# Latents' queries and keys turned by VectorE and transfers, zeros of the experts' rows moved into the context steps

## Chip, cores and metric

One core of a Trainium2 chip runs one program for one layer. The metric is device time of the run in microseconds (us), as the median of several runs. Everything is float32. The engines are named as the profile names them: PE is TensorE (PEld its weight loads), DVE is VectorE, ACT is ScalarE, POOL is GpSimd, SP is SyncE, whose queue issues nearly all transfers (SPq in the profile).

## What is computed

A perceiver layer with 256 latents `x` of 512 channels and 4096 context tokens: attention of the latents over context and themselves, then a state-space block, then a mixture of experts.

```python
x = x + xattn(layernorm(x), ctx)     # 16 heads, 4 key/value heads, head size 128
x = x + ssd(layernorm(x))            # state-space block
x = x + experts(layernorm(x))        # 32 experts, the best 6 for each token, and a shared one

# xattn, with x already normed:
q, k, v = x @ wq, x @ wk, x @ wv                 # by heads
k_ctx, v_ctx = ctx @ wk_ctx, ctx @ wv_ctx
q, k = rope(rms_norm(q, q_w)), rope(rms_norm(k, k_w))
k_ctx = rms_norm(k_ctx, k_w)                     # no rope
scores = q @ concat(k_ctx, k).T / sqrt(128)      # causal among the latents
out = softmax(scores) @ concat(v_ctx, v) @ wo
```

## The kernel before

**Attention is held turned.** A score product takes a block of 128 keys, `kT` (128 channels on the partitions, 128 keys), as the stationary side and the queries of four heads, `qT` (128 channels, 4 x 128 queries), as the moving side. Projections give rows by token: `ps_self` for the latents, `ps_k` and `ps_kv` for the context. So each 128 x 512 block of queries or keys has to be turned, head by head, before it can be used.

**Two arms.** A small test of the norms' weights selects between `layer(lctx, True)` (`bounded`: scores are small enough for an exponential without a running maximum) and a general arm. With the inputs of this case the bounded arm runs, and only it is meant below.

**First stage, to about 84 us.** After the loads of the first weights come the projections of context block 0 (four pieces of 128 tokens; `ctx_k`, `ctx_v`, turned by `ctx_t`) and of the latents: two blocks of keys (`k_of`), two of values (`self_value`) and eight of queries (`q_of`: four groups of four heads, j, by two blocks of 128 latents, t). The tuple that begins in L486 writes their order out by hand. `self_block` makes one block of keys or queries: `project` on TensorE into `ps_self`; in `norm_rope` a copy `raw` by ACT (L432), squares for the norm on ACT (`head_squares`, L247), four VectorE operations for the rotation (L437 to L440), a power on VectorE and POOL (`power_half`, L188 and L189), and a multiplication by POOL (L441) into `o`, which lies in the room of `lacc`. `self_block` returns a function `turn` (L467, L468) that turns `o` by four TensorE transposes into one PSUM bank `selfT` and copies it by ACT into `qT` or `kT0`. Turns are called later, when more than two are waiting in the list `turns`; the last ones are called three scores into the attention.

**Buffers.** In the bounded arm the pool `ps_tp` has one PSUM bank (tag `tp`), used by the turns of the latents (`selfT`) and of context block 0 (`kTp`). The SBUF pool `krp` has two buffers for each tag. Tag `sq` is shared by the squares, which nobody reads (only their sums are used), and by `tr` of the context keys.

**Context steps.** `bounded_attention` goes through s = 0 to 8. Step 0 is the latents' attention to themselves (12 scores; query block 1 sees both key blocks). After the last score of a group the queries are scaled in place by ACT (L597). Steps 1 to 8 are attention to context blocks 0 to 7, with 32 scores each. Each score is a product `scT` (L542), an exponential on ACT to `prT` (L545), a sum on VectorE (L553) and, two scores later, a value product `oT` (L562). On the diagonal of step 0 VectorE also masks `prT` (L548). Beside the scores of step s the keys and values of the next context block are made: `fast_steps(s)` returns 14 pieces, those of `row(1)` and then those of `row(0)`, and `bounded_attention` spreads them evenly over the scores. Two pieces of each row end with `key_blocks`, which turns a finished block of context keys without TensorE: VectorE turns all 32 x 32 blocks in one instruction (L284), four transfers put them into DRAM (`kd`, L286), each block at its turned place, and a fifth reads `kT` back (L288).

**Zeros.** The experts' rows are gathered in DRAM in `xg`, whose unused rows must be zero, and parts of `ye` and `ye2` must be as well. `clear(n)` writes a seventh of `xg` from a zeroed row block of `xn` (L501); `clear(0)` also the parts of `ye` and `ye2` (L505). `clear(s - 1)` is called at the beginning of step s.

**Order.** The instructions of an engine run in the order that a scheduler lays down while compiling: by priority, which follows the program's order, among those that its own estimate of times takes as ready. An instruction that has nothing to wait for can so come far ahead of its place in the program: the zeros are called in steps 1 to 7, and SP issues them from 31.8 to 79.1 us. `tc.keep_in_program_order(i)` puts i behind the instruction that the program has last given to the same engine.

Of the kernel before, what the change touches and what calls it, by code (L numbers as in the profile page):

```python
# [11 lines left out]
FP = mybir.dt.float32  # L12
# [7 lines left out]
P = 128  # L20
L = 256
NT = L // P
DM = 512
# [4 lines left out]
NH = 16  # L28
NKV = 4
REP = NH // NKV  # L30
HD = 128
# [9 lines left out]
SH = 16  # L41
# [5 lines left out]
NE = 32  # L47
# [9 lines left out]
TAIL = 6  # L57
# [10 lines left out]
def perceiver_layer(ctx: ExitStack, tc: tile.TileContext, a: dict, out: bass.AP):  # L68
    nc = tc.nc
    V, S, G, TE = nc.vector, nc.scalar, nc.gpsimd, nc.tensor  # L70
# [48 lines left out]
    xg = tc.dram_tile((ROUNDS * NE * P, DM), FP, name="xg")  # L119
    ye = tc.dram_tile(((NE + 1) * P, DM), FP, name="ye")  # L120
    ye2 = tc.dram_tile(((NE + 1) * P, DM), FP, name="ye2")
    kd = [tc.dram_tile((CK // P, NKV, HD, P), FP, name=f"kd{c}") for c in range(NC)]
    sums_d = [tc.dram_tile((SH, P), FP, name=f"sums{t}") for t in range(NT)]

    rope = const.tile([P, NT, 2, HALF], FP, name="rope")
# [7 lines left out]
    def layer(ctx, bounded):  # L133
# [6 lines left out]
        xn = keep.tile([P, NT, DM], FP, name="xn")  # L140
# [67 lines left out]
        def project(ps, lhs, rhs_of):  # L208

            for k in range(KD):  # L210
                TE.matmul(ps, lhs(k), rhs_of(k), start=(k == 0), stop=(k == KD - 1))  # L211
# [8 lines left out]
        krp = pool("krp", 2)  # L220
        ps_tp = pool("ps_tp", 1 if bounded else 2, space=PSUM)
# [19 lines left out]

        def head_squares(raw):

            sq = krp.tile([P, REP, HD], FP, tag="sq", name="sq")
            ss = small.tile([P, REP], FP, tag="ss", name="ss")
            for h in range(REP):
                S.activation(sq[:, h, :], raw[:, h, :], AF.Square, accum_out=ss[:, h:h + 1])  # L247
            return ss

        def key_rms(raw, r):  # L250

# [10 lines left out]
        def context_tiles(c):  # L262

            kT = kvp.tile([P, NKV, CK], FP, tag="kT", name="kT")
            v = kvp.tile([P, CK // P, NKV * HD], FP, tag="v", name="v")
            r = small.tile([P, CK // P, NKV], FP, tag="rk", name="rk", bufs=2)
            kv[c + 1] = (kT, v, r)
            raws = {}

            def key_transpose(i):  # L270
                tp = ps_tp.tile([P, NKV, P], FP, tag="tp", name="kTp")
                raw = raws.pop(i)
                for h in range(NKV):
                    TE.transpose(tp[:, h, :], raw[:, h, :], ident)

                if bounded:
                    S.copy(kT[:, :, i * P:(i + 1) * P], tp)
                else:
                    S.activation(kT[:, :, i * P:(i + 1) * P], tp, AF.Copy, scale=kw_col)

            def key_blocks(i):

                tr = krp.tile([P, NKV * HD], FP, tag="sq", name="tr")
                V.transpose(tr, raws.pop(i).rearrange("p h d -> p (h d)"))  # L284
                for b in range(0, P, 32):
                    nc.sync.dma_start(kd[c][i, :, :, b:b + 32].rearrange("h (j a) k -> a h j k", a=32),  # L286
                                      tr[b:b + 32, :].rearrange("a (h j k) -> a h j k", h=NKV, k=32))
                nc.sync.dma_start(kT[:, :, i * P:(i + 1) * P], kd[c][i].rearrange("h d k -> d h k"))  # L288
            return v, r, raws, key_transpose, key_blocks

        def context_pieces(c):
# [137 lines left out]
        def norm_rope(ps, t, tb):  # L429
# [11 lines left out]
            G.tensor_tensor(o, o, r.unsqueeze(2).to_broadcast([P, REP, HD]), ALU.mult)  # L441
            return o

        kT0 = kvp.tile([P, NKV, CK], FP, tag="kT", name="kT0")
        v0 = kvp.tile([P, CK // P, NKV * HD], FP, tag="v", name="v0")
        kv[0] = (kT0, v0, None)
# [12 lines left out]
        def self_block(t, w, tb, dst):  # L459
            ps = ps_mm.tile([P, 512], FP, tag="mm", name="ps_self")  # L460
            project(ps, lambda k: xT[:, k, t * P:(t + 1) * P], lambda k: w[:, k, :])
            o = norm_rope(ps.rearrange("p (h d) -> p h d", d=HD), t, tb)

            def turn():
                tp = ps_tp.tile([P, REP, P], FP, tag="tp", name="selfT")
                for h in range(REP):
                    TE.transpose(tp[:, h, :], o[:, h, :], ident)  # L467
                S.copy(dst, tp)  # L468
            return turn
# [24 lines left out]

        G.memset(xn[:, 0, :], 0.0)

        def clear(n):

            per = -(-ROUNDS * NE // (NC - 1))
            e0, e1 = n * per, min((n + 1) * per, ROUNDS * NE)  # L500
            nc.sync.dma_start(xg[e0 * P:e1 * P, :].rearrange("(e p) d -> p e d", p=P),  # L501
                              xn[:, 0:1, :].to_broadcast([P, e1 - e0, DM]))
            if n == 0:
                for y in (ye, ye2):
                    nc.sync.dma_start(y[(NE - TAIL) * P:, :].rearrange("(e p) d -> p e d", p=P),  # L505
                                      xn[:, 0:1, :].to_broadcast([P, TAIL + 1, DM]))

        nc.sync.dma_start(by_channel, a["by_channel"])
        nc.sync.dma_start(by_head, a["by_head"].partition_broadcast(P))
# [16 lines left out]
        def bounded_attention(beside):  # L526
# [50 lines left out]
            for s in range(NC + 1):  # L577
                if s < NC:
                    steps = [(s, g, t, i) for g in range(NKV) for t in range(NT) for i in range(len(keys_of(s, t)))]
                else:  # L580
                    steps = [(s, g, t, i) for t in range(NT) for g in range(NKV) for i in range(len(keys_of(s, t)))]
                    last_weights()
                extra = []
                if 0 < s < NC:
                    if s + 1 < NC:
                        load_ctx(s + 1)
                    clear(s - 1)
                    extra = fast_steps(s)
                done = 0
                for n, st in enumerate(steps):  # L590
                    if s == 0 and n == 3:
                        for turn in turns:
                            turn()
                    pending.append((*st, scores(*st)))
                    if s == 0 and st[3] == len(keys_of(s, st[2])) - 1:
                        q = qT[:, st[2], heads4(st[1]), :]
                        S.activation(q, q, AF.Copy, scale=kw_col)  # L597
                    if len(pending) > 2:
                        values(*pending.pop(0))
                    if s < NC:  # L600

                        while done < min(len(extra), len(extra) * (n + 1) // (len(steps) - 4)):
                            extra[done]()
                            done += 1
                    elif n > len(steps) // NT + 1:
                        for f in beside():
                            f()
# [103 lines left out]
        m = {}  # L711
# [6 lines left out]
        def mamba_memory():  # L718
            m["lm"], = carve(ctxp.tile([P, CK // P, KD, P], FP, tag="ctx", name="lm"), (SH, P))
            m["w_bcd"], = carve(ctxp.tile([P, CK // P, KD, P], FP, tag="ctx", name="w_bcd"), (KD, CK))  # L720
            nc.sync.dma_start(m["w_bcd"][:, :, 0:272], a["W_inT"][:, 2048:2320].rearrange("(k p) n -> p k n", p=P))
            for t in range(NT):
                m["csT", t] = krp.tile([P, REP, HD], FP, tag="sq", name="csT")[0:SH, 0, :]
            off = [krp.tile([P, REP, HD], FP, tag="kn", name="off") for _ in range(2)]
            m["off"] = ring([o.rearrange("p h d -> p (h d)") for o in off])
            gu = krp.tile([P, REP, HD], FP, tag="kraw", name="gu")
            m["sh"] = krp.tile([P, REP, HD], FP, tag="kraw", name="sh").rearrange("p h d -> p (h d)")
            for t, (tag, shape) in enumerate((("kT", [P, NKV, CK]), ("v", [P, CK // P, NKV * HD]))):
                tl = kvp.tile(shape, FP, tag=tag, name=f"xc{t}")
                names = ("vdt", "nab", "u", "z", "z2", "ser", "dt", "dA", "acs", "ea", "decay", "e1")  # L730
                m["xc", t], *sm = carve(tl, (XCT, P), *[(SH,)] * len(names))
                m.update({(n, t): v for n, v in zip(names, sm)})
                m["gu", t] = gu[:, t, :]
                m["kv", t] = tl
            m["xraw"], = carve(lacc[:, 0], (XCT, P + CONV - 1))
            m["zs"] = wvc.rearrange("p (t k) n -> p t (k n)", t=NT)
            m["xt"] = wkc.rearrange("p (t k) n -> p t (k n)", t=NT)
            m["xdt"], = carve(ctx0, (NT, DI))

            m["xdd"], m["s0"], m["y", 0], m["yT", 0] = carve(qT, (DI,), (DI,), (DI,), (DIT, P))  # L740
            m["y", 1], m["yT", 1] = carve(qT, (DI,), (DIT, P))
            G.memset(m["xraw"][:, :, 0:CONV - 1], 0.0)
            S.activation(m["ea", 0], a_log, AF.Exp)
# [522 lines left out]
        with ExitStack() as rctx:  # L1266
# [37 lines left out]
            for n in range(NP):  # L1304
# [27 lines left out]
                else:  # L1332
                    e0 = 2 * n - (NE - TAIL)
# [95 lines left out]
```

## Time and profile before

| | us |
|---|---|
| median of 3 runs | 1018.16 (1018.09 to 1018.35) |
| the profiled execution, its own time | 1019.19 |
| its span in the profile | 1017.40 |
| TensorE busy | 996.1 (98%) |
| VectorE busy | 495.4 (49%) |
| ACT busy | 384.6 (38%) |
| POOL busy | 156.9 (15%) |

The granted TensorE clock is full throughout (0.998). The span is cut into 40 slices of 25.4 us; the first four hold the loads, the latents' projections and step 0, the context steps follow up to slice 28, then the state-space block and the experts. In the lists of instructions, `x40` means that 40 of a kind are counted together; "idle before" names what ended the time in which the engine stood still. Starts are microseconds from the start of the span.

### The profile page before, as it was taken

How to read it: one execution, taken by the hardware profiler on the slowest of the kernel's cores; microseconds unless marked ns; L12 is line 12 of the kernel's file. 1: busy time of each engine (PE TensorE's matmuls, PEld its weight loads, DVE VectorE, ACT ScalarE, POOL GpSimd, SP SyncE). 2: the span in 40 equal slices, each digit the busy share in tenths (PEclk: the TensorE clock that was granted, in tenths of full speed). 3: DMA queues.
4: the chain of work that ended last, by engine and by line, in shares of the span. 5: the costliest groups of instructions: out<-in, count | busy, mean ns of one | idle time of the engine just before them, and what ended most of it. 6: DMA issues, size and time to landing. Idle time of an engine off the chain costs nothing.

```text
span 1017.4 us, 9099 instructions
## 1 busy us (share of the span) xinstructions
PE 996.1 (98%) x2818; PEld 480.9 (47%) x2818; DVE 495.4 (49%) x975; ACT 384.6 (38%) x870; POOL 156.9 (15%) x156
## 2 busy tenths in 40 slices
PE   7999999999999999999999999999999999999997
PEld 3444444444444444444444444444656554555553
DVE  4347454445444454544544544575885653322233
ACT  3456444443443443443443434442445431222210
POOL 4343001001001101100200200000131322000022
PEclk9999999999999999999999999999999999999999
DMA  9997021110210301301301202500264358999833
GB/s 335 375 404 303 0 42 50 34 31 30 64 26 16 83 11 32 82 10 32 83 2 40 63 0 42 156 10 0 94 200 148 114 208 318 357 353 371 291 116 95
DMA packets 115435, 127.73 MB, mean 126 GB/s; under 512 B 63377, under 2 KB 78642, under 8 KB 114226
## 3 DMA queue, kind: packets, MB, share of 16 engines
q1 hardware_dynamic: 108272, 111.52, 33.9%
q0 software_dynamic: 2208, 8.39, 2.3%
q10 hardware_dynamic: 4898, 7.16, 1.9%
q8 instruction: 24, 0.39, 0.2%
q14 instruction: 33, 0.27, 0.1%
HBM read 88.76 MB, written 38.29 MB: 125 GB/s over the span
## 4 chain that ended last, share of the span: by engine, by line
PE 91%; DMA 2%; DVE 2%; POOL 2%; issue 1%; ACT 1%; SPq 0%; POOLq 0%; DVEq 0%; ACTq 0%
PE oT L562 23%; PE scT L542 22%; PE ps_kv L350 17%; PE ps_egu L211 7%; PE ps_self L211 3%; PE ps_ye L1256 2%; PE ps_o L754 2%; PE ps_ye L1259 1%; PE ps_v L211 1%; PE ps_k L211 1%; PE ps_xbc L211 1%; PE ps_out L944 1%; PE xgTp L1201 1%; PE total L1247 1%; DMA lm<-sums 1%
## 5 line engine op out<-in xcount | busy, mean ns | idle before, releaser
L553 DVE TENSOR_TENSOR lacc<-lacc,prT 128x512 f32<-128x512 f32 x260 | 182.7, 704 | 246.3 <-ACT prT L545 245.5
L545 ACT ACTIVATE prT<-scT,bq,rk 128x512 f32<-128x512 f32 x256 | 198.3, 775 | 228.0 <-PE scT L542 223.1
L562 PE MATMUL oT<-prT,v 128*128 128x512 f32 x536 | 272.2, 592 | 1.3 <-DVE prT L548 1.3
L542 PE MATMUL scT<-qT,kT 128*128 128x512 f32 x536 | 272.3, 592 | 0.0
L562 PEld LDWEIGHTS oT<-prT,v 128*128 128x128 f32 x536 | 101.7, 190 | 129.4 <-issue 109.3
L542 PEld LDWEIGHTS scT<-qT,kT 128*128 128x128 f32 x536 | 101.2, 190 | 124.6 <-issue 123.1
L189 POOL TENSOR_TENSOR rk<-pv,mhalf 128x4 f32<-128x4 f32 x32 | 32.3, 1011 | 357.8 <-DVE pv L188 357.1
L247 ACT ACTIVATE sq<-kraw 128x128 f32<-128x128 f32 x128 | 38.3, 301 | 94.0 <-DVE kraw L368 93.9
L1216 DVE TENSOR_TENSOR hid<-si,ps_egu 128x128 f32<-128x128 f32 x32 | 9.2, 288 | 94.2 <-ACT si L1214 94.2
L350 PE MATMUL ps_kv<-fast,fast 128*128 128x512 f32 x112 | 52.6, 592 | 0.0
L350 PE MATMUL ps_kv<-wkv,fast 128*128 128x512 f32 x112 | 52.6, 592 | 0.0
L350 PE MATMUL ps_kv<-wkv,ctx 128*128 128x512 f32 x112 | 52.6, 592 | 0.0
L568 DVE TENSOR_TENSOR oacc<-oT,oacc 128x512 f32<-128x512 f32 x64 | 43.7, 683 | 0.0
L1170 POOL DMA_INDIRECT yk<-ye,row_y x12 | 13.3, 1105 | 137.5 <-PE ps_egu L211 134.1
L350 PEld LDWEIGHTS ps_kv<-wkv,ctx 128*128 128x128 f32 x112 | 21.3, 190 | 26.8 <-issue 23.7
L350 PEld LDWEIGHTS ps_kv<-fast,fast 128*128 128x128 f32 x112 | 21.3, 190 | 26.8 <-issue 21.8
L350 PEld LDWEIGHTS ps_kv<-wkv,fast 128*128 128x128 f32 x112 | 21.3, 190 | 26.8 <-issue 23.4
L1262 ACT COPY y_sb<-ps_ye 128x512 f32<-128x512 f32 x26 | 15.2, 586 | 48.8 <-PE ps_ye L1259 43.0
L368 DVE TENSOR_TENSOR kraw<-ps_kv,fast 128x256 f32<-128x256 f32 x42 | 17.9, 425 | 31.6 <-PE ps_kv L350 31.6
L1214 ACT ACTIVATE si<-ps_egu 128x192 f32<-128x192 f32 x32 | 10.6, 332 | 58.5 <-PE ps_egu L211 58.5
L754 PE MATMUL ps_o<-wo,qT 128*128 128x512 f32 x64 | 28.8, 592 | 0.0
L211 PE MATMUL ps_self<-wq,xT 128*128 128x512 f32 x64 | 28.6, 592 | 0.0
(294 smaller groups left out, 1129.6 us busy)
## 6 DMA issues: line engine op xcount, KB each, us to landing
xg<-xn SPq DMA_DIRECT2D x6, 2560.0 KB, 21.5
w_in<-in_pairs_dram SPq DMA_DIRECT2D x14, 768.0 KB, 6.9
ctx<-in_ctxT_dram SPq DMA_DIRECT2D x7, 1024.0 KB, 5.0
kd<-tr SPq DMA_DIRECT2D x112, 64.0 KB, 2.4
kT<-kd SPq DMA_DIRECT2D x28, 256.0 KB, 2.8
xg_sb<-xg SPq DMA_DIRECT2D x28, 256.0 KB, 6.3
ye<-y_sb ACTq DMA_DIRECT2D x26, 256.0 KB, 7.1
wkv<-in_pairs_dram SPq DMA_DIRECT2D x6, 768.0 KB, 6.8
```

The costliest lines, as they stand in the source:

```text
L189: return G.tensor_tensor(dst, v[:, :n], mhalf[:, :n], ALU.pow)
L211: TE.matmul(ps, lhs(k), rhs_of(k), start=(k == 0), stop=(k == KD - 1))
L247: S.activation(sq[:, h, :], raw[:, h, :], AF.Square, accum_out=ss[:, h:h + 1])
L350: TE.matmul(ps, lhs(k), rhs(k), start=(start and k == 0), stop=(k == 1), skip_group_check=True)
L368: V.tensor_tensor(to[n], ps[:, n, :], more[:, n, :], ALU.add)
L542: TE.matmul(sc, kT[:, g, i * P:(i + 1) * P], qT[:, t, heads4(g), :].rearrange("p h q -> p (h q)"), start=True, stop=True)
L545: S.activation(pr, sc, AF.Exp, bias=shift, scale=SCALE if r is None else r[:, i, g:g + 1])
L553: V.tensor_tensor(la, la, pr, ALU.add)
L562: TE.matmul(outs[g, t], v[:, i, g * HD:(g + 1) * HD], pr, start=(n == 0), stop=last)
L568: V.tensor_tensor(ov, outs.pop((g, t)), ov, ALU.add)
L754: TE.matmul(m["ps_o", t], aT[:, t, h, :], wo[j][:, h % 4, :], start=(h == 0), stop=(h == NH - 1))
L1256: TE.matmul(ps[i], h[:, i, :], wd[:, i, :], start=True, stop=False)
```

## The change

It has three parts.

1. `self_block` no longer turns its block on TensorE (bounded arm). It calls the new `turn_heads`, which is what `key_blocks` did so far: one VectorE transpose of 128 x 512, four writes to DRAM (`qd`, ten new tiles, one for each block of latents' keys or queries) and one read into `kT0` or `qT`.
2. The squares of `head_squares` go to a PSUM tile with the tag `tp`; the tag `sq` of `krp` becomes `tr` and holds only blocks turned by VectorE (and, after the attention, `csT`).
3. `clear(s - 1)` is no longer called at the beginning of step s but as a fifteenth piece in the middle of the step's pieces, and its transfers are held in the program's order on SP.

```diff
+    blocks_d = [tc.dram_tile((REP, HD, P), FP, name=f"qd{i}") for i in range(NT * (1 + NH // REP))]
...
         def head_squares(raw):
-            sq = krp.tile([P, REP, HD], FP, tag="sq", name="sq")
+            sq = ps_tp.tile([P, REP, HD], FP, tag="tp", name="sq")
...
+        def turn_heads(dst, src, by):
+            tr = krp.tile([P, REP * HD], FP, tag="tr", name="tr")
+            V.transpose(tr, src.rearrange("p h d -> p (h d)"))
+            for b in range(0, P, 32):
+                nc.sync.dma_start(by[:, :, b:b + 32].rearrange("h (j a) k -> a h j k", a=32),
+                                  tr[b:b + 32, :].rearrange("a (h j k) -> a h j k", h=REP, k=32))
+            nc.sync.dma_start(dst, by.rearrange("h d k -> d h k"))
...
             def key_blocks(i):
-                tr = krp.tile([P, NKV * HD], FP, tag="sq", name="tr")
-                V.transpose(tr, raws.pop(i).rearrange("p h d -> p (h d)"))
...
+                turn_heads(kT[:, :, i * P:(i + 1) * P], raws.pop(i), kd[c][i])
...
+        qd = list(blocks_d)
...
             o = norm_rope(ps.rearrange("p (h d) -> p h d", d=HD), t, tb)
+            if bounded:
+                return turn_heads(dst, o, qd.pop())
...
+        zeros = lambda to, z: tc.keep_in_program_order(nc.sync.dma_start(to, z))
         def clear(n):
...
-            nc.sync.dma_start(xg[...], xn[...])
+            zeros(xg[...], xn[...])
...
                 if 0 < s < NC:
                     if s + 1 < NC:
                         load_ctx(s + 1)
-                    clear(s - 1)
                     extra = fast_steps(s)
+                    extra.insert(len(extra) // 2, lambda: clear(s - 1))
...
-                m["csT", t] = krp.tile([P, REP, HD], FP, tag="sq", name="csT")[0:SH, 0, :]
+                m["csT", t] = krp.tile([P, REP, HD], FP, tag="tr", name="csT")[0:SH, 0, :]
```

More of the change, by code (lines that the diff above doesn't have):

```diff
@@ L281, in key_blocks @@
             def key_blocks(i):
-                tr = krp.tile([P, NKV * HD], FP, tag="sq", name="tr")
[L284 to L288, printed above, removed]
+                turn_heads(kT[:, :, i * P:(i + 1) * P], raws.pop(i), kd[c][i])
             return v, r, raws, key_transpose, key_blocks
@@ L500, in clear @@
             e0, e1 = n * per, min((n + 1) * per, ROUNDS * NE)
-            nc.sync.dma_start(xg[e0 * P:e1 * P, :].rearrange("(e p) d -> p e d", p=P),
-                              xn[:, 0:1, :].to_broadcast([P, e1 - e0, DM]))
+            zeros(xg[e0 * P:e1 * P, :].rearrange("(e p) d -> p e d", p=P),
+                  xn[:, 0:1, :].to_broadcast([P, e1 - e0, DM]))
             if n == 0:
                 for y in (ye, ye2):
-                    nc.sync.dma_start(y[(NE - TAIL) * P:, :].rearrange("(e p) d -> p e d", p=P),
-                                      xn[:, 0:1, :].to_broadcast([P, TAIL + 1, DM]))
+                    zeros(y[(NE - TAIL) * P:, :].rearrange("(e p) d -> p e d", p=P),
+                          xn[:, 0:1, :].to_broadcast([P, TAIL + 1, DM]))
         nc.sync.dma_start(by_channel, a["by_channel"])
```

## The prediction

> **What bounds the kernel now.** I read the page first, then TensorE's waits, then the tile selfT, then the timeline of 30 to 200 us engine by engine.
>
> From the page: busy shares, and the DMA row of the 40 slices (25.4 us each).
> ```profile
> PE 996.1 (98%) x2818; PEld 480.9 (47%) x2818; DVE 495.4 (49%) x975; ACT 384.6 (38%) x870; POOL 156.9 (15%) x156
> DMA  9997021110210301301301202500264358999833
> ```
> TensorE (PE) is the bound nearly everywhere: an instruction taken from it shortens the run, unless a wait takes its place. The DMA engines are full in slices 1 to 3 only because of weight loads and zeros; from 109 to 149 us their share is 0.11.
>
> From TensorE's waits and from the tile selfT, the turned blocks that the change touches (min/median/max ns):
> ```profile
> PE oT L562 <- DVE prT L548: 1.3, 1, 1.3
> PE selfT L467 <- POOL lacc L441: 0.6, 2, 0.3
> L467 PE MATMUL selfT<-ident,lacc x40: 272/273/329, 34.5 to 89.9; 128*128 128x128 f32 x40
> L468 ACT COPY qT<-selfT x8: 586/591/593, 46.8 to 90.2; 128x512 f32<-128x512 f32 x8
> ```
> Ten blocks of four TensorE transposes, in 34 to 90 us. TensorE has only two waits worth naming here.
>
> From the timeline of TensorE, around the end of this stage (start us, duration):
> ```profile
> 83.62 0.60 PE L467 MATMUL selfT<-ident,lacc 128*128 128x128 f32 x4
> 84.06 2.74 PE L542 MATMUL scT<-qT,kT 128*128 128x512 f32 x6
> 88.08 1.12 PE L562 MATMUL oT<-prT,v 128*128 128x512 f32 x2 [1.28 <-DVE prT L548]
> 89.54 0.66 PE L467 MATMUL selfT<-ident,lacc 128*128 128x128 f32 x4 [0.33 <-POOL lacc L441]
> 90.03 1.02 PE L542 MATMUL scT<-qT,kT 128*128 128x512 f32 x2
> ```
> One block holds TensorE from 83.62 to 84.06: 0.44 us, although one transpose is listed with 273 ns (they overlap). The first value product waits for VectorE.
>
> From the timeline of all engines: why VectorE is late there.
> ```profile
> 81.16 1.74 POOL L344 TENSOR_TENSOR fast<-ctx 128x512 f32<-128x512 f32 x1
> 81.69 1.49 DVE L438 TENSOR_TENSOR lacc<-raw,oacc 128x256 f32<-128x256 f32 x1
> 83.11 1.49 DVE L439 TENSOR_TENSOR lacc<-raw,oacc 128x256 f32<-128x256 f32 x1
> 84.52 2.31 DVE L188 TENSOR_SCALAR pv<-ss 128x4 f32<-128x4 f32 x1
> 86.75 0.68 DVE L440 TENSOR_TENSOR lacc<-lacc 128x512 f32<-128x512 f32 x1
> 87.35 0.68 DVE L548 TENSOR_TENSOR prT<-prT,upper 128x512 f32<-128x512 f32 x1
> ```
> L438 takes 1.49 us here and 0.42 elsewhere: each VectorE instruction ends when a POOL one ends. From 80.39 (ACT's copy of the last projection) to 88.03 this chain is gapless, and TensorE waits behind it.
>
> The path that the change copies exists already for context keys; its timeline, and the row of the zeros:
> ```profile
> 143.00 0.71 DVE L284 STREAM_TRANSPOSE tr<-kraw 128x512 f32<-128x512 f32 x1
> 145.24 1.03 SPq L286 DMA_DIRECT2D kd<-tr  x2
> 148.64 0.38 SPq L288 DMA_DIRECT2D kT<-kd  x1
> L501 SPq DMA_DIRECT2D xg<-xn x7: 452/6282/6607, 31.8 to 79.1; - x7
> ```
> The read at 148.64 lands 2.9 us later: 7.8 us from the end of the block transpose (143.7) to the turned keys (151.5). One 2.5 MB write of zeros occupies SP for about 6.3 us, with the DMA engines full.
>
> [...] The trace agrees on one (273 ns) but shows 0.11 us of TensorE each when four follow one another; I use that. [...] all 28 block transposes take 0.70 to 0.71 us, one of them (179.15) beside a POOL instruction. [...] 31.7 us in 23 waits of L288 on kd<-tr.
>
> **The change part by part.**
> *Removed from TensorE.* Ten groups at 0.435: 4.35 us, and the waits of 0.29 (before the group at 76.26) and 0.33 (before 89.54). Ten ACT copies of 0.59 go as well; ACT was not waited for here, so they give nothing.
> *What of it reaches the end.* Nine groups and 0.29 lie ahead of the wait at 88.08, so TensorE gets there 9 x 0.435 + 0.29 = 4.2 us earlier. But the chain that releases it hangs on the last projection (ends 80.19), ahead of which lie eight groups and 0.29: 3.77 us. So the wait grows by 0.43, and the product moves by 3.77 less what block transposes add to the chain. Only the ninth block's can fall into it (its input is ready at 81.20). It costs 0.70 if it stands between L188 and L440, nothing if it fills time in which L438 waits for POOL: I take 0.2. Behind the product the tenth group and its wait go: 0.44 + 0.33 = 0.77. **Sum: 3.77 - 0.2 + 0.77 = 4.3 us.**
> *Added to VectorE.* 10 x 0.705 = 7 us, where VectorE is busy 9.3 of 26 us (32 to 58) and 14.8 of 26 (58 to 84). Covered, except as above.
> *Added to SP and DMA.* 40 writes at 0.49 and 10 reads at 0.38, 23 us of SP in some 55, and 5 MB of transfers. SP stands still for each read until its four writes have landed (2.4 us); behind it are the next block's writes and loads of wo, which are needed only at 700 us. The self keys are ready near 45 us and needed at 80. The last query block decides: product on POOL done at 89.48 - 3.77 + 0.2 = 85.9, turn about 87.5 with up to 0.9 of queueing on VectorE, landed 7.8 later: 95.3. It is needed by the eleventh of the 12 scores of step 0, at 102.05 before, now 97.7. Slack 2.4 us; cost 0, upper bound 3 if the scheduler's SP order puts another wait ahead of it.
> *Squares into a PSUM bank.* 168 ACT squares of 0.297; no ACT write to PSUM is in the trace. [...] Twice as long would be 16 x 0.3 = 4.8 us per context step of some 79, with ACT busy 16 of 40: hidden either way, 0. But the one bank is shared with the four turns of context block 0 (22.8, 24.2, 27.2, 42.3 us). Earlier squares end at 20.6 and 40.9, so it is free; only if the squares of the next block get the bank first do the turns at 27.2 and 42.3 wait 2.4 us each. Bounds 0 and 4.8; I take 0, since ready work comes first.
> *Zeros.* Away from 31 to 93 us, where they would stand in front of the new transfers; now behind the first pair of key blocks of each context step, in step 1 from about 149. 6.3 us each, the first with ye and ye2 about 15 us (6.2 MB at the 0.41 MB/us of the row above): to 165. SP's next work is the context load at 172.67 and the second pair's writes from 174.03. Cost 0 while that gap of 25 us holds; no gain is possible, as TensorE waits for none of these transfers.
> *Pacing.* A step has 15 pieces instead of 14 over 28 scores, so products of the second row come up to one score and value (1.72 us) later; the last stays. Its key 0 landed at 187.5 and was needed at 193.9, key 2 at 183.8 and 189.6: slack some 6 us. Cost 0, bounds -0.5 and +0.5 per step, taken as independent.
>
> **The rivals.** *A, the sum holds (0.68):* saved 3.6 to 5.3, 4.3 likeliest. *B, a new wait for the last block (0.14):* its queries land 1.5 to 3 us late behind SP's or VectorE's queue; saved 1.3 to 2.8, about 1016. For it: SP's chain of 7.8 us; against: slack 2.4. *C, nothing to measure (0.09):* the bank or the chain on VectorE takes nearly all of it, saved under 1.5, about 1017.5. *D, slower (0.09):* zeros reach the queue late in the step and key blocks 2 and 0 land behind them. One mechanism, at the start of the next step: a delay of 6.3 (15 in step 1) against a slack of 6, so with the writes' own queueing some 9 us once and 1 to 2 in five steps, +16 - 4.3: about 1030. It begins when zeros are still queued some 6 us past 174; against it, they only need to be issued within 25 us. That the transposes stay on TensorE is excluded, as this case runs the bounded arm (selfT and key blocks in the trace).
>
> **How the numbers follow.** The profiled execution took 1019.19 (span 1017.40 and 1.8 around it), the median is 1018.16, 1.0 less; the sum is a difference and goes on both: span about 1013.1 in the profile, median 1013.9. Cases A, B and C reach from 1012.4 to 1017.4, leaving out D and the edges. A difference of 0.2% (2.0 us) is about what can be told from none. Faster by more: A and some 0.09 of B, 0.77; within: the rest of B and C, 0.14; slower: D, 0.09.
>
> **What would show it.** Right: no selfT rows, 10 more block transposes of 0.70, first score near 80 us, the first value product near 84.5 with a wait of 1.7 to 2.4 on L548, the first context product near 104.5 instead of 108.92, and an unchanged distance from there to the end. B: TensorE waits for qT<-qd before 105 us. C: turns of context block 0 waiting for squares. D: waits of scT for kT<-kd early in steps 2 to 8. The prediction is wrong if the distance behind 110 us changes by over 1 us.

## The result, and the profile after

The kernel after takes **1027.14 us** (median of 6 runs, 1024.47 to 1028.5), the kernel before, run beside it, 1018.25: ratio 1.0084, 95% interval 1.0070 to 1.0097. It is slower by 8.9 us, where 4.3 us less were forecast. Its profiled execution took 1025.46 us (span 1023.7), 6.3 more than that of before.

The page of after: busy shares, the granted clock and the DMA share of the 40 slices.

```profile
PE 994.2 (97%) x2778; PEld 477.1 (47%) x2778; DVE 503.5 (49%) x985; ACT 391.5 (38%) x860; POOL 154.7 (15%) x156
PEclk9999899999999999999999999999999999999999
DMA  9634216313304304304304203500254368999833
```

The 40 TensorE transposes are gone (2818 to 2778 matmuls), VectorE has its ten instructions more, the zeros have left slices 2 to 4. But slice 5 (102 to 128 us) has an 8 in the clock row, which no slice of before has.

TensorE's waits, after (us in total, times, longest):

```profile
PE scT L552 <- DMA qT<-qd: 5.5, 1, 5.5
...
PE oT L572 <- DVE prT L558: 2.1, 3, 1.4
PE scT L552 <- ACT qT L607: 1.5, 1, 1.5
...
PE oT L572 <- ACT prT L555: 0.9, 1, 0.9
```

The first is the mechanism of rival B of the prediction, at more than its size: TensorE waits for a query block that comes back from DRAM. The timeline of TensorE shows where (score products are L552, value products L572, a score is two instructions):

```profile
79.48 2.74 PE L552 MATMUL scT<-qT,kT 128*128 128x512 f32 x6
82.67 1.12 PE L572 MATMUL oT<-prT,v 128*128 128x512 f32 x2 [0.46 <-DVE prT L558]
...
99.01 1.10 PE L552 MATMUL scT<-qT,kT 128*128 128x512 f32 x2 [1.48 <-ACT qT L607]
105.59 4.40 PE L552 MATMUL scT<-qT,kT 128*128 128x512 f32 x6 [5.49 <-DMA qT<-qd]
```

Step 0 starts earlier, as forecast (79.48 against 84.06), and its first value product hardly waits. Then the eleventh score, first user of the last query block, starts at 105.59 us. The six instructions that begin there take 4.40 us; the six at 79.48 take 2.74.

The wait of 1.48 us at 99.01 belongs to the same mechanism. The tenth score, first user of the ninth block, starts there. The profile puts its wait down to ACT, whose L607 ended at 98.87; but in wo_behind, below, this score starts ahead of that ACT instruction, and in t_only (0.32 us) and sq_back (2.60 us) its wait is put down to `qT<-qd`. So the ninth block was late as well.

Why the last block is late, first on VectorE and POOL (timeline of all engines, these two picked; L445 makes the last block, L254 is its block transpose):

```profile
83.56 1.04 POOL L445 TENSOR_TENSOR lacc<-lacc,r 128x512 f32<-128x512 f32 x1
84.81 1.75 DVE L558 TENSOR_TENSOR prT<-prT,upper 128x512 f32<-128x512 f32 x1
86.48 0.68 DVE L576 COPY oacc<-oT 128x512 f32<-128x512 f32 x1
87.08 1.16 DVE L563 TENSOR_TENSOR lacc<-lacc,prT 128x512 f32<-128x512 f32 x1
88.16 1.75 DVE L558 TENSOR_TENSOR prT<-prT,upper 128x512 f32<-128x512 f32 x1
89.33 1.71 POOL L349 TENSOR_TENSOR fast<-ctx,fast 128x512 f32<-128x512 f32 x1
89.94 1.71 DVE L561 COPY lacc<-prT 128x512 f32<-128x512 f32 x2
...
92.78 0.69 DVE L254 STREAM_TRANSPOSE tr<-lacc 128x512 f32<-128x512 f32 x1
```

The block is ready at 84.60, but on VectorE its transpose stands behind masks (L558), sums and copies of the attention. A mask takes 1.75 us at 84.81 and at 88.16, while POOL makes sums of the context rows (L346 to L349, 84.56 to 91.04), and 0.68 at 91.58, behind them; the block transposes take 0.69 to 0.71 everywhere, at 83.00 beside POOL's L190 (82.10 to 83.48) as well. The mask reads two SBUF tiles, the block transpose one, but one input alone does not decide it: a copy L561 takes 1.26 us at 83.62, beside POOL's L445, and 0.43 at 82.65, beside L190. That POOL lengthens the masks is my reading of these times; which VectorE instructions it lengthens, and why, they do not show. In before, L438 took 0.41 to 0.42 us in seven of ten and 1.26 to 1.49 in three; the three instructions that the prediction put down to POOL (L438, L439, L188) ended 0.03 to 0.28 us behind one of POOL's, the two long masks here 0.55 behind one.

Then on SP's queue (timeline of SP):

```profile
85.16 10.40 SPq L256 DMA_DIRECT2D qd<-tr  x4
95.72 0.38 SPq L258 DMA_DIRECT2D qT<-qd  x1
96.14 1.05 SPq L256 DMA_DIRECT2D qd<-tr  x2
97.29 0.49 SPq L183 DMA_DIRECT2D wo<-in_wo_dram  x1
99.76 0.38 SPq L258 DMA_DIRECT2D qT<-qd  x1
100.19 1.09 SPq L183 DMA_DIRECT2D wo<-in_wo_dram  x2
```

The first line is two writes of the ninth block, a long wait, and two writes of the tenth. The read of a block stands behind the first two writes of the next one, so the ninth block, turned at 83.70, is read at 95.72 only, behind the tenth's turn: on this queue a transfer at the head that waited held up one behind it that needed nothing more (without the tenth block ahead of it the same read was issued at 88.41, in l1_wo_14 below). The last read (99.76) has a 1 MB load of `wo` ahead and two behind. From the chain that ended last:

```profile
99.76 5.69 DMA qT<-qd
```

It lands at 105.45. From the end of the block transpose (93.48) to the queries that is 12.0 us; the context keys took 7.8.

The windows of after (busy us and count of PE, PEld, DVE, ACT, POOL; granted clock; DMA share; GB/s) show the second loss:

```profile
95.00:100.00 5.00, 3.52 (x8) 1.06 (x6) 1.92 (x4) 1.98 (x3) 0.00 (x0) 1.00 0.68 134
100.00:105.00 5.00, 0.11 (x1) 0.00 (x0) 2.41 (x4) 4.12 (x5) 0.00 (x0) 0.70 1.01 325
105.00:110.00 5.00, 4.41 (x7) 2.06 (x8) 0.00 (x0) 0.82 (x2) 0.00 (x0) 0.62 0.83 315
110.00:115.00 5.00, 5.00 (x13) 2.13 (x13) 3.65 (x7) 3.15 (x5) 0.00 (x0) 1.00 0.01 2
```

During and after the long wait the granted clock is 0.70 and 0.62 on the average of 5 us. Windows of 0.5 us show two levels, 1.00 and 0.50, but for those at the two ends of the slow stretch (0.97 and 0.70):

```profile
102.00:102.50 0.50, 0.00 (x0) 0.00 (x0) 0.02 (x1) 0.50 (x2) 0.00 (x0) 0.50 0.91 269
108.00:108.50 0.50, 0.50 (x2) 0.21 (x1) 0.00 (x0) 0.00 (x0) 0.00 (x0) 0.50 1.02 397
```

It was 0.50 from about 102.0 to 108.8 us: from inside the wait, which lasted from 100.1 to 105.6, to 3.2 us behind its end.

**The whole difference in one account.** From the first product `lnT`, at 18.52 us before and 18.28 after, up to the first product with `wo`, at 694.30 and 700.69, time is busy plus idle time of TensorE. Windows of before, then of after:

```profile
18.52:694.30 675.78, 673.88 (x1618) 300.90 (x1616) 339.78 (x559) 286.88 (x661) 98.40 (x85) 1.00 0.27 80
```
```profile
18.28:700.69 682.41, 672.26 (x1577) 297.14 (x1576) 347.34 (x569) 293.34 (x651) 97.02 (x85) 0.99 0.31 87
```

Idle time goes from 1.90 to 10.15: **+8.25**. Busy time should have fallen by ten groups, 4.35, to 669.53; it is 672.26: **2.7 more**. Slow clock is most of it: the six instructions at 105.59 alone are 4.40 - 2.74 = 1.7. Another 0.3 to 0.6 stands also in kernels whose clock is full in this stretch (table below), so it is an error of this account; the rest was not traced. Together 8.25 + 2.7 - 4.35 = +6.6, less the 0.2 by which after reaches `lnT` earlier: +6.4, as measured. From there to the end both take 323 us.

### The profile page after: what moved, and what is told of

It is laid out like the page before. It is cut to its first block, busy times and chain, and to the rows that moved or that the text cites. A ratio compares the mean times of both kernels' runs of the same rounds, so it can differ in the third digit from the quotient of the medians.

```text
span 1023.7 us, 9074 instructions
## 1 busy us (share of the span) xinstructions
PE 994.2 (97%) x2778; PEld 477.1 (47%) x2778; DVE 503.5 (49%) x985; ACT 391.5 (38%) x860; POOL 154.7 (15%) x156
## 4 chain that ended last, share of the span: by engine, by line
PE 90%; DVE 3%; DMA 2%; ACT 1%; POOL 1%; issue 1%; SPq 0%; DVEq 0%; POOLq 0%; ACTq 0%
PE oT L572 22%; PE scT L552 22%; PE ps_kv L354 16%; PE ps_egu L212 7%; PE ps_self L212 3%; PE ps_ye L1266 2%; PE ps_o L764 2%; PE ps_v L212 2%; PE ps_k L212 2%; PE ps_xbc L212 1%; PE ps_ye L1269 1%; PE ps_out L954 1%; PE xgTp L1211 1%; PE total L1257 1%; PE ps_yd L894 1%
## 5 line engine op out<-in xcount | busy, mean ns | idle before, releaser
L563 DVE TENSOR_TENSOR lacc<-lacc,prT 128x512 f32<-128x512 f32 x260 | 185.8, 715 | 235.7 <-ACT prT L555 234.7
L552 PE MATMUL scT<-qT,kT 128*128 128x512 f32 x536 | 272.6, 596 | 7.0 <-DMA qT<-qd 5.5
L572 PE MATMUL oT<-prT,v 128*128 128x512 f32 x536 | 271.8, 593 | 3.2 <-DVE prT L558 2.1
L552 PEld LDWEIGHTS scT<-qT,kT 128*128 128x128 f32 x536 | 101.9, 191 | 134.1 <-issue 131.6
L572 PEld LDWEIGHTS oT<-prT,v 128*128 128x128 f32 x536 | 101.3, 190 | 132.6 <-issue 116.0
L190 POOL TENSOR_TENSOR rk<-pv,mhalf 128x4 f32<-128x4 f32 x32 | 32.3, 1010 | 374.8 <-DVE pv L189 374.8
L248 ACT ACTIVATE sq<-kraw 128x128 f32<-128x128 f32 x128 | 35.6, 278 | 45.2 <-DVE kraw L372 43.1
```

The source lines that it names most:

```text
L190: return G.tensor_tensor(dst, v[:, :n], mhalf[:, :n], ALU.pow)
L552: TE.matmul(sc, kT[:, g, i * P:(i + 1) * P], qT[:, t, heads4(g), :].rearrange("p h q -> p (h q)"), start=True, stop=True)
L563: V.tensor_tensor(la, la, pr, ALU.add)
L572: TE.matmul(outs[g, t], v[:, i, g * HD:(g + 1) * HD], pr, start=(n == 0), stop=last)
```

## The experiments

**Theory 1:** the last query block lands too late, because its block transpose is late on VectorE and its read late on SP; the wait also costs clock. Theory 2: the zeros delay key blocks (the rival "slower" of the prediction). Theory 3: the squares' PSUM bank holds up turns. In the table, "idle" is TensorE's idle time from the first `lnT` (near 18 us) to the first product with `wo`; "busy above the sum" is its busy time in that stretch, less 673.88, plus 0.435 for each group taken off TensorE. "Half clock" is the time in it with a granted clock of 0.50, added up from windows of 0.5 us around the place where windows of 5 us show less than 0.97.

| kernel | blocks through DRAM | median, us | ratio to before (95%) | idle, us | busy above the sum, us | half clock, us |
|---|---|---|---|---|---|---|
| before | 0 | 1018.2 to 1018.7 | 1 | 1.90 | 0 | 0 |
| after | 10 | 1027.14 | 1.0084 (1.0070 to 1.0097) | 10.15 | 2.7 | 6.8 |
| z_only | 0 | 1018.93 | 1.0007 (0.9998 to 1.0016) | 2.81 | 0.3 | 0 |
| t_only | 10 | 1023.23 | 1.0049 (1.0032 to 1.0066) | 7.95 | 3.5 | 6.8 |
| sq_only | 0 | 1022.99 | 1.0044 (1.0029 to 1.0059) | 4.43 | 1.8 | 3.4 |
| sq_back | 10 | 1025.83 | 1.0068 (1.0053 to 1.0084) | 11.21 | 2.5 | 10.2 |
| wo_behind | 10 | 1024.76 | 1.0056 (1.0039 to 1.0073) | 7.59 | 4.7 | 3.4 + 3.4 |
| t_early_wo | 10 | 1019.33 | 1.0005 (0.9996 to 1.0014) | 4.55 | 0.6 and 2.3 | 0 and 3.4 |
| only_last_sb | 1 | 1023.09 | 1.0045 (1.0028 to 1.0062) | 5.20 | 1.7 | 3.4 |
| l4_pe | 6 | 1016.99 | 0.9982 (0.9975 to 0.9989) | 2.38 | 0.5 | 0 |
| l2_pe | 8 | 1015.46 | 0.9973 (0.9962 to 0.9984) | 2.62 | 0.6 | 0 |
| l2_t14 | 8 | 1015.62 | 0.9971 (0.9959 to 0.9983) | 1.71 | 0.3 | 0 |
| l1_wo_14 | 9 | 1015.83 | 0.9973 (0.9961 to 0.9984) | 2.99 | 0.6 | 0 |

The last column holds what is easily missed: the clock falls to half for 3.4 us, or for two or three times 3.4. By an estimate from these 3.4 us and the clock of 0.50, each such stretch takes up to 1.7 us of work (measured in after: 4.40 instead of 2.74 us for six instructions), less where TensorE stands still in it anyway.

### The parts one by one: z_only, t_only, sq_only, sq_back

z_only is before with part 3 alone:

```diff
+        zeros = lambda to, z: tc.keep_in_program_order(nc.sync.dma_start(to, z))
...
-                    clear(s - 1)
                     extra = fast_steps(s)
+                    extra.insert(len(extra) // 2, lambda: clear(s - 1))
```

> Only the zeros are moved; queries, keys and squares as before. Theory 1 (the last two query blocks come back from DRAM too late, TensorE waits for them and then runs at a lower clock): 1018.2, within 1 us of before. Theory 2 (zeros delay the second pair of key blocks in each step): most of the 9 us, 1025 to 1028, with TensorE waiting for kT<-kd. Theory 3 (squares in PSUM hold up TensorE's turns of context block 0): 1018.2.

Measured 1018.93, no difference that counts. **Theory 2 falls** as the cause of the loss: TensorE has no wait for `kT<-kd`, here or in after. One wait is new among its waits:

```profile
PE oT L564 <- ACT prT L547: 0.9, 1, 0.9
```

t_only is after with the zeros as before (at the beginning of a step, not held in the program's order):

> The turning through DRAM and the squares in PSUM stay, the zeros are called at the beginning of a step again and not pinned. Theory 1: as after, 1024 to 1029, with a wait of 5 us for qT<-qd near 100 us. Theory 2: the loss goes, 1013 to 1015. Theory 3: as after.

Measured 1023.23. The wait for `qT<-qd` is there in full (5.4 us at 105.08, idle 7.95): the turning alone makes the kernel slower. By the ratios it is 3.6 us faster than after, so beside the turns the move of the zeros has a price that z_only does not show. In the traces t_only has 2.2 us less idle time: 0.9 of it is the new wait of z_only, 1.2 the shorter wait for the ninth block (0.32 instead of 1.48). The rest of the 3.6 is not settled by these two traces.

sq_only is before with part 2 alone:

```diff
-            sq = krp.tile([P, REP, HD], FP, tag="sq", name="sq")
+            sq = ps_tp.tile([P, REP, HD], FP, tag="tp", name="sq")
```

> Only the squares go to the PSUM bank; all blocks of the latents are turned by TensorE as before, so the bank has ten more users than after. Theory 1 and 2: 1018.2 within 1 us. Theory 3: 1021 or more, with TensorE's transposes waiting for squares.

Measured 1022.99, slower by 0.44%. Its TensorE timeline:

```profile
73.60 0.65 PE L467 MATMUL selfT<-ident,lacc 128*128 128x128 f32 x4 [1.60 <-POOL lacc L441]
89.64 1.13 PE L562 MATMUL oT<-prT,v 128*128 128x512 f32 x2 [1.56 <-DVE prT L548]
92.03 1.11 PE L467 MATMUL selfT<-ident,lacc 128*128 128x128 f32 x4 [1.27 <-POOL lacc L441]
```

Where the latents are turned by TensorE, the squares and the turns share the bank, and two turns wait, 1.60 and 1.27 us; before had 0.3 there. The profile names POOL's product as what ends the wait; that the bank is behind it is inferred from the edit, which changes nothing else, and not shown by the trace. With waits of 1.56 and 1.27 the granted clock was 0.66 from 90 to 95 us (0.50 for 3.4 us). In after those turns are gone, so this cost can't be the cause there. The converse shows it, sq_back, after with the squares in SBUF:

```diff
-            sq = ps_tp.tile([P, REP, HD], FP, tag="tp", name="sq")
+            sq = krp.tile([P, REP, HD], FP, tag="tr", name="sq")
```

> The kernel after with only the squares put back into SBUF, where they share the two buffers of the tag tr with the turned blocks. Theory 1 (the squares' place has no part in the loss): the last block transpose and the read stay as late as in after, wait for qT<-qd 5 us, time 1025 to 1029. Rival a (the squares in the PSUM bank delay context block 0's turns, as they delayed TensorE's turns in the kernel with only the squares moved): 1021 to 1024. Rival b (the squares now wait for buffers that transfers still read): 1030 or more, with ACT waiting for DMA.

Measured 1025.83, runs of 1025.15 to 1027.14, in the span of after's runs; two of TensorE's waits name the transfer, one for the ninth block and one for the tenth:

```profile
99.05 1.56 PE L552 MATMUL scT<-qT,kT 128*128 128x512 f32 x2 [2.60 <-DMA qT<-qd]
106.85 4.27 PE L552 MATMUL scT<-qT,kT 128*128 128x512 f32 x6 [6.24 <-DMA qT<-qd]
```

**Theory 3 falls** as a cause of after's loss; theory 1's range held.

### The last blocks back on TensorE: l2_pe, l4_pe, l1_wo_14, l2_t14

l2_pe is after with an argument `pe` that sends chosen blocks to TensorE:

```diff
-            if bounded:
+            if bounded and not pe:
                 return turn_heads(dst, o, qd.pop())
...
-        q_of = lambda j, t: self_block(t, wq[j], tab_q, qT[:, t, REP * j:REP * (j + 1), :])
+        q_of = lambda j, t: self_block(t, wq[j], tab_q, qT[:, t, REP * j:REP * (j + 1), :], pe=j == 3)
```

> After, but the two query blocks of the last group of heads (j = 3) are turned by TensorE again. Theory 1: the wait and the low clock go; eight blocks of 0.435 are saved, 3.5 us, so 1014 to 1016. Theory 2: 1023 to 1027, little changed. Theory 3: little changed.

Measured **1015.46**, faster than both kernels. The wait for DRAM is gone; what stays is one wait for a turn:

```profile
PE selfT L474 <- POOL lacc L445: 1.3, 1, 1.3
```

The same with `pe=j >= 2`, six blocks through DRAM:

> The kernel after, with the four query blocks of groups j = 2 and 3 turned by TensorE again; six blocks go through DRAM. Theory 1: no wait for qT<-qd; six groups at 0.435 us are saved, 2.6 us, and the squares in the PSUM bank that four of TensorE's turns need now cost some: 1015.5 to 1018 us, so no better than the kernel with only the two blocks of j = 3 on TensorE (1015.46). Rival (each block through DRAM costs time of its own, fewer are better): under 1015 us.

Measured 1016.99. By the ratios it lies 0.9 us above l2_pe; two groups more on TensorE are 0.87. That agrees with the price of a group, and with a block through DRAM costing nothing by itself; the intervals of the two ratios leave about 1 us open.

l1_wo_14 returns only the very last block (`pe=j == 3 and t == 1`), with the loads of `wo` behind the last read and the zeros joined to the seventh piece:

> Only the very last query block is turned by TensorE, nine go through DRAM; the loads of wo are issued behind the last read through DRAM; zeros joined to the seventh piece as in l2_t14. Theory 1 (only a block that has no time left after its turn costs a wait): the ninth block's turn is at about 88 us and lands near 96, just when needed or up to 1 us late; 9 groups x 0.435 saved, less than 1 us of new wait: 1013.5 to 1015.5 us. Rival (the queue backs up already for the ninth block): wait for qT<-qd over 2 us, time 1016 or more.

Measured 1015.83, no wait for `qT<-qd`. The ninth block is turned at 83.00 as in after, but is read at 88.41 instead of 95.72, as no tenth block stands ahead of its read: it was late only through the last one. So one block decides. The ninth group that it takes off TensorE (0.44 less than l2_t14) is eaten by idle time (2.99 against 1.71).

l2_t14 is l2_pe with the zeros joined to the seventh of 14 pieces, `(f(), clear(s - 1))`:

> The kernel after with the two query blocks of group j = 3 turned by TensorE again (as in l2_pe), and the zeros no longer a piece of their own but joined to the seventh of a step's 14 pieces: the same place, the pacing of before. Theory 1: the wait of 0.9 us for ACT's prT near 655 us, which l2_pe, after and the kernel with only the zeros moved all have, comes from the 15-piece pacing and is gone here: 1014 to 1015 us, against 1015.46 of l2_pe. Rival (the wait comes from the zeros' transfers or from somewhere else): the wait stays and the time is 1015.2 to 1015.8.

The wait for ACT's `prT` is gone (it lies at 670.55 us in after, 665.16 in z_only, not near 655 as the expectation had it), and idle time is 0.9 shorter. So the 15-piece pacing makes it (the zeros stay where they were). The median, 1015.62, is the same as l2_pe's: 0.9 us less of idle time could not be seen in the time.

### All ten through DRAM, but in time: wo_behind, t_early_wo

wo_behind leaves VectorE's order and moves only the loads of `wo`, behind `read[0]`, which `self_block` sets to the read that `turn_heads` now returns:

```diff
-        wo = [wpiece(a["wo"][j * 512:(j + 1) * 512, :], f"wo{j}") for j in range(3)]
+        with tc.issue_after(read[0].ins) if bounded else ExitStack():
+            wo = [wpiece(a["wo"][j * 512:(j + 1) * 512, :], f"wo{j}") for j in range(3)]
```

> The kernel after, with one edit: the three loads of wo (1 MB each) are issued behind the read of the last query block instead of around it; the order on VectorE and TensorE is that of after. Theory 1 (the last query block arrives late; of its 12.0 us from the end of the block transpose to landing about 4 us are the queue and the traffic of the wo loads, the rest of the lateness is the block transpose at 92.8 us instead of 87.5): the read lands 2.5 to 3.5 us after its issue instead of 5.7, TensorE's wait for qT<-qd falls from 5.5 to about 2.7 us, the time falls by 2.5 to 5 us to 1022 to 1025 us (the more, the less the granted clock falls after the shorter wait). Rival (the wait is set by something else on the way, [...] and wo lies beside it): wait still 5 us or more, time 1026 to 1028.

The chain of waits of this kernel:

```profile
92.83 0.63 DVE tr L254
...
98.33 2.61 DMA qT<-qd
...
101.08 3.60 PE scT L555 x4
```

The read lands in 2.61 us instead of 5.69: the loads of `wo` were 3 us of it. The whole trip, from 93.46 to 100.94, is 7.5 us, against 7.8 of the context keys. The wait falls from 5.5 to 2.4, and the one for the ninth block is gone: its read is issued at 94.47, since a write that occupied SP for 1.71 us in after's trace (at 93.85) takes 0.49 here and in t_only; why is not known. The time, 1024.76, came near the weak end of the expectation: TensorE has a new wait of 1.93 us for ACT's copies (L333), and the clock fell twice, once by either wait (0.66, 0.78, 0.88 from 100 to 115 us).

t_early_wo is wo_behind, and lets the attention's instructions from the fourth score of step 0 be issued only behind the last block transpose (`turned[0]`):

```diff
+            last_turn = turned[0].ins
...
+                    late = ExitStack()
+                    if s == 0 and n > 2:
+                        late.enter_context(tc.issue_after(last_turn))
                     pending.append((*st, scores(*st)))
...
+                    late.close()
```

> As wo_behind, and in addition the attention's instructions of step 0 from its fourth score on may be issued only after the last block transpose, so that on VectorE the last block transpose stands at place 93 instead of 97, directly behind what its input needs. All ten blocks still go through DRAM, squares and zeros as in after. Theory 1: the last block transpose runs at 86 to 90 us instead of 92.78, its queries land at 94 to 98.5, TensorE's wait for qT<-qd is under 1 us, the granted clock stays near 1.00 from 100 to 110 us, and the time is 1014 to 1017 us: the saving of 4.3 us is there once the last block is in time. Rival (ten blocks through DRAM cost about 8 us by their own traffic or by a lower clock, whatever the order): 1021 or more, with no wait for qT<-qd. Third case: the exponentials and masks that now come later hold up TensorE's value products by 1 to 3 us: 1017 to 1020.

The last block transpose ran at 88.24, the read at 93.81, and there is no wait for `qT<-qd`. The trace kept had a span of 1015.9 us, 1.5 less than before; but the median of 12 runs is 1019.33 (1016.31 to 1020.43): nothing gained, in the range of the third case. Two waits stand where the others were: 0.99 for VectorE's `oacc` at 93.10, which is new, and 1.93 for ACT's copies at 102.14, as in wo_behind. A second trace of the same kernel:

> The same kernel as t_early_wo once more, for a second trace: its profiled run had a span of 1015.9 us, but its median was 1019.3. Theory 1 (in its slower runs the granted clock falls after the waits of 1.0 and 1.9 us near 93 and 102 us): at a span of over 1017.5 us this trace shows a granted clock under 0.9 in one stretch of 5 us between 90 and 115 us, and at 1016 or less none. Rival: the slower runs lose their time elsewhere, with full clock there.

Its span is 1017.0, between the two cases of the expectation; the waits up to the first product with `wo` are the same (idle 4.55 in both). The windows of the first trace, then of the second:

```profile
100.00:105.00 5.00, 3.07 (x8) 1.43 (x8) 2.14 (x5) 4.12 (x7) 0.00 (x0) 1.00 0.97 374
105.00:110.00 5.00, 5.00 (x13) 2.15 (x12) 4.53 (x8) 2.23 (x3) 0.00 (x0) 1.00 0.01 2
```
```profile
100.00:105.00 5.00, 3.07 (x7) 1.12 (x6) 1.99 (x4) 4.05 (x6) 0.00 (x0) 0.85 1.03 388
105.00:110.00 5.00, 5.00 (x10) 2.11 (x10) 3.06 (x6) 2.18 (x4) 0.00 (x0) 0.80 0.11 42
```

Same program, same waits, 3.07 busy in the first window; but the second has clock 0.85 and 0.80 (at a level of 0.50 that is 3.5 us, by an estimate from these two windows from about 103.5 to 107.0), and its first context block transpose starts at 137.20 instead of 134.84. Of these 2.36 us, 0.66 are there from the start: `lnT` comes at 19.01 instead of 18.35, the first score at 80.21 instead of 79.55. The other **1.7 us are clock alone**, half of 3.4. The second trace's end makes 1.3 of it good, with a shorter wait for `hidS` near the end (0.7 instead of 2.0). How much of the slower runs' time is clock stays open: the mean clocks recorded for the 12 runs do not follow their times (0.998 at 1020.43 us, 0.997 at 1017.72).

### The last block alone through DRAM: only_last_sb

Nine blocks and the keys on TensorE (`pe=not (j == 3 and t == 1)`), squares in SBUF, zeros as in after:

> The reverse: of the ten blocks only the last query block goes through DRAM, the nine others are turned by TensorE as before; squares in SBUF as before; zeros in the middle of the steps as in after. Its block transpose is not behind the sums of context on VectorE as far as in after, and the loads of wo are issued long before. Saved on TensorE: 0.44 + 0.33 us. Theory 1 (what decides is the time at which the last block lands): block transpose near 91 us (its product on POOL ends at 89.5 as before), landed 7.8 us later at about 99, needed at about 101.3: wait 0 to 1 us, time 1017 to 1018.5 us. Rival (a round trip of that block costs a wait of 5 us and a low clock whatever else is in the queues): 1022 to 1026.

Measured 1023.09, a miss for theory 1 and, in its mechanism, for the rival: no wait for `qT<-qd` at all. VectorE's timeline:

```profile
86.21 0.68 DVE L444 TENSOR_TENSOR lacc<-lacc 128x512 f32<-128x512 f32 x1
88.90 0.71 DVE L254 STREAM_TRANSPOSE tr<-lacc 128x512 f32<-128x512 f32 x1 [2.02 <-POOL lacc L445]
89.54 0.65 DVE L558 TENSOR_TENSOR prT<-prT,upper 128x512 f32<-128x512 f32 x1
```

and TensorE's:

```profile
90.24 1.13 PE L572 MATMUL oT<-prT,v 128*128 128x512 f32 x2 [3.98 <-DVE prT L558]
```

Here the block transpose stands ahead of the first mask. It waits 2.02 us for POOL, the mask behind it waits along, and TensorE for the mask, 3.98 us (1.28 before); clock 0.66 from 90 to 95. Too early on VectorE costs as well, 4.6 us by the ratio: TensorE's turn had not touched VectorE at all.

## Why the prediction was wrong

**Right:** ten groups at 0.435, nearly: in the kernels with full clock the busy time falls by 0.35 to 0.39 us for each group moved, 0.3 to 0.6 us short of the sum in all. The first score came at 79.48 ("near 80"), the selfT rows are gone, the block transposes take 0.70, the last block is ready on POOL at 84.6 (85.9 forecast). The zeros, from 153.7 us on, cost nothing when moved alone (z_only). The squares' bank did not hold up context block 0's turns: among TensorE's waits there is none for them, only two of their weight loads waited for squares, 1.3 us together. An ACT square into PSUM takes 278 to 281 ns on the average instead of 301 to 303 into SBUF.

**Wrong, the step "the last query block decides": "turn about 87.5 ... landed 7.8 later: 95.3 ... cost 0, upper bound 3".** Three terms failed.
- *The turn.* It ended at 93.48: 6.0 late. I allowed 0.9 for the queue. VectorE's order was taken as that of before with block transposes put in; it was laid anew, and eight attention instructions came ahead of this one, 8.2 us long, several of them longer than elsewhere beside POOL's sums (two masks of 1.75 us instead of 0.68). t_early_wo shows the turn at 88.24, with five of them put behind it.
- *The trip.* 12.0 instead of 7.8. I counted the loads of `wo` as behind the blocks' chain and needed late; that they stood in front of the last read and beside it was not priced. wo_behind: 3 of these 4.2 us, and another 1.2 are the one long write at 93.85.
- *The consequence.* Landing at 105.5 is 10.2 us later than forecast; TensorE, itself 2.4 later than forecast by smaller waits (1.48 of them for the ninth block), stood still for 5.5.

**Wrong, the first value product.** A wait of 1.7 to 2.4 and 84.5 us were forecast; it came at 82.67 with 0.46. The chain that releases it was taken over from before, but on VectorE it became 1.2 us shorter: from L442 to the mask 4.46 us in after, from L438 to the mask 5.66 before.

```profile
77.47 1.26 DVE L442 TENSOR_TENSOR lacc<-raw,oacc 128x256 f32<-128x256 f32 x1
81.93 0.69 DVE L558 TENSOR_TENSOR prT<-prT,upper 128x512 f32<-128x512 f32 x1
```

Beside it POOL has two instructions of together 3.6 us (L445, L334), where before had three of 5.7. No block transpose fell into the chain; the ninth stands behind the mask, at 83.00. The gain was real, but not forecast: luck of the new order. TensorE's order was laid anew too: the first context product, forecast near 104.5, came at 91.79, in the middle of step 0.

**Missing, the clock.** No step had a price for a wait beyond its length. In after's profile it was 1.7 us at least. After's median lies 1.7 above its profiled run; the recorded mean clock is 0.995 in that run and in the one faster run, 0.992 to 0.994 in the four slower ones, which points to more slow clock there, but no trace of such a run was kept.

**Wrong, "unchanged distance behind 110".** It changed by 1.2 us between the first context block transpose (142.46, 5.2 late) and the first product with `wo` (700.69, 6.4 late); 0.9 is the pacing's wait, which the prediction put at 0 with bounds of 0.5 per step.

**The rivals.** B had the mechanism with a wait of 1.5 to 3 us; it was 5.5, and 1.5 for the ninth block. D, the only slower one, had the wrong mechanism. The chance of 0.09 for slower had no case for the block that I had called decisive.

**Left open:** why the compiled order puts the last turn so late, why one write held SP for 1.71 us, and why the same waits lower the clock in one run and not in another.

## What to carry to other kernels

When work moves off the busiest engine onto a chain through other engines and DRAM, ask which item of it has no work left behind it to hide the trip, and leave that item where it was: with eight or nine of ten blocks moved the kernel gained 2.8 us; with all ten it was 11 us slower than that. An instruction added to VectorE had two costs here, what it waited behind (8.2 us of attention instructions in after) and what waited behind it (a mask, and TensorE for 3.98 us, in only_last_sb); price both from that engine's queue near the point of need, and don't take the old order for granted. In a queue like SP's, look also for a finished item behind an unfinished one (the ninth block, turned at 83.70 and read at 95.72). Waits of TensorE of one to a few us cost, beyond their length, some 1.7 us of clock in several of these runs (the second trace of t_early_wo), once or more often, and none in others (1.3 us in before and l2_pe).

## What was not expected of the hardware

The granted clock fell after waits much shorter than after's 5.5 us: after 1.56 and 1.27 us within 4 us (sq_only, 0.66 from 90 to 95), after 2.4 (wo_behind, 0.66 from 100 to 105), and after 0.99 and 1.93 in one of two runs (t_early_wo, 0.85 from 100 to 105 in the second trace). It stayed at 1.00 after a wait of 1.3 (before, l2_pe). The slow stretch began inside a wait (after: 102.0, in the wait from 100.1 to 105.6) or about 1 us behind its end (only_last_sb: the wait ends at 90.24, the two instructions there take 1.13 us (before's at 88.08: 1.12), those at 91.21 take 1.61 instead of 1.02), and it lasted 3.4 us or a multiple in every trace that has one (6.8 in after, from 102.0 to 108.8; the others in the table). In sq_only, wo_behind and t_early_wo every wait near it was shorter than the stretch (2.4 us at most).
